# A hand-ordered attention kernel on one core: projections moved ahead of ranks in the front, two score banks lent to projections, rotary factors made later and in two parts, output-weight loads moved

## The chip, the cores and the metric

The kernel runs on one core of one Trainium2 chip. The metric is device time in microseconds (us), the median of several executions. A core has five engines that run side by side, each in its own program order: TensorE (PE) for matrix products, VectorE (DVE), ScalarE (ACT) and GpSimd (POOL) for elementwise work, and SyncE (SP), which here only issues transfers. Transfers (DMA) are issued by an engine's queue and carried by 16 DMA engines. An instruction that waits holds back everything behind it on its engine.

## What is computed

The state x is 64 x 32 x 512, that is 2048 rows of 512 floats, all float32. Four layers are added to it in turn. In outline, with the names of the reference:

```python
def _L0_cond_ref(x, condition, weights):          # channel mix, 32 x 32 per batch
    W = weights[condition]
    return jnp.einsum('bct,bcd->bdt', x, W)
def _L1_cond_ref(...):                            # linear 512 -> 512, plus rank-16 adapters
    result = jnp.einsum('bsd,od->bso', x, base_weight) + base_bias
    h = jnp.einsum('bsd,brd->bsr', x, lora_A_w[adapter_ids])
    return result + jnp.einsum('bsr,bor->bso', h, lora_B_w[adapter_ids])
def _L2_cond_ref(...):                            # attention over a paged cache
    q, k, v = x @ Wq.T, x @ Wk.T, x @ Wv.T        # 32 query heads, 8 key heads, D = 128
    q, k = _rope(_rmsnorm(q, q_norm_w), pos), _rope(_rmsnorm(k, k_norm_w), pos)
    k_all = concatenate([k_cache[block_table], k]); v_all = ...     # 512 + 32 keys
    return (softmax(mask(q @ k_all.T)) @ v_all) @ Wo
x = x + L0(x); x = x + L1(x); x = x + L2(x); x = x + L0(x, other weights)
```

## The kernel before

**Tiles.** The rows are cut into 16 tiles `t` of 128 rows (4 batches of 32). The key heads are cut into two groups `g` of four. A step is one (g, t), so there are 32 steps; two steps with neighbouring t make a `Pair` (16 pairs). A unit is one batch of one step (128 units), and a slot is one key head of one unit: 512 slots, numbered from 0. The work ahead of the first scores has negative slots, from -43 on.

**The order is written by hand.** A plan says for each slot what is recorded there: `at(slot, where, what)`, where `where` is one of fetch, pool, pe, power, turn, dve, keep, act, store. `slot(i)` (L1157 on) records these lists in a fixed order, and each engine runs its instructions in the order in which they are recorded. Around the lists stand the slot's own scores, the transposes of slot i-2 (`flip`) and the products with the values of slot i-3:

```python
run(i, "pe")
run(i, "power")
norm_piece(i)
...
run(i, "turn")
...
run(i, "dve")
norm_piece(i)
norm_piece(i)
run(i, "keep")
```

So in a slot all "pe" products come before all "turn" transposes, and "power" and "dve" are mostly VectorE work. There is no scheduler behind it.

**The front (slots -43 to 0).** `First` carries tile t through the first two layers, with home = -39 + 2t:
- `diagonal` (DVE, home-2) spreads the gathered 32 x 32 channel weights into `mix_diag`; `mix` (PE, home-1) is the channel mix; `add` adds it to x.
- `turn_a`, `keep_a` (home-1, even t): the adapter rows are transposed (aT, L441) and copied by ACT. `turn_x`, `keep_x` (home): x is transposed into x1T (PE) and copied (ACT, L457). `bias` (POOL, home+1).
- `ranks` (PE, home+1) makes h = aT x1T; `own_ranks` (DVE) masks it; `linear` makes the five products into `l_ps`: chunks 0, 1, 2 at home+1, chunks 3 and 4 (the adapter's) at home+2; a second `add` (DVE, L433).
- `turn_out`, `keep_out` (home+3): x2T, the operand of the projections. `sums` (DVE, home+4, odd t) are four sums and differences of a pair's two x2T.
- Beside it, `Turn` transposes the key pages of group 0 ("page turns", 16 of them), `angles()` makes sines and cosines in pieces (`more`: the trig pieces), two a slot, and `rotary(t)` (slots -32 to -17, one tile each) multiplies them by the norm weights into a table in HBM of 256 KB a tile; `v_rows` and `key_f` (row numbers and positions of the cache) are made after slot -38. `rot` has two buffers.

**Projections.** The projections of a pair (keys and values, then query blocks 0 and 1) are written as seven products of sums for each block (`Block.ORDER`), each product two matmuls of 128x128 by 128x512 (L634). Each goes to one PSUM bank (pool `ps_m`, tag m, one buffer); `take` on DVE (L646) adds it to a `raw` tile and frees the bank. Pair i has home = 32(i-1) - 1, products in home to home+30; pair 0 has home -33. For the first pair of a group, `block_sum` (DVE) makes sums of the weights beside it. `Norm` then does RMSNorm, the rotary products (`straight`, `swapped`, L721) and the transposes. `load_rotary` (L579, SP queue, home+6) loads the two tables of a pair.

**Scores and values.** The scores take a pool of two PSUM banks, `ps_s`, first used in slot 0. A unit's keys, `kT`, come in 16 loads of one page, 64 KB each (L777, SP queue), issued at slot 4(u-1) for unit u, into one of two buffers. Its values `v_sb` come by four gathers on POOL's queue; `pen` (POOL, L792) is the mask.

**The end.** In the last pair's slots (home 447) `load_o_weights` (L206) loads the output weights on POOL's queue, eight weights in two halves of 512 KB each; `fetch_o` loads stored attention outputs (o_in: a11, a12, a21, a22, two halves of 512 KB each) from slot 478 on, for three products of the output projection that are done within the last slots. After the last slot, PE does the rest of the output projection (L1283) and the second channel mix (L1301).

## Time and profile before

| | us |
|---|---|
| median of 3 runs | 2508.31 (2504.9 to 2513.72) |
| profiled execution, its time | 2507.74 |
| its span (mean TensorE clock 0.995 of full) | 2506.0 |
| first scores start | 212.81 |
| last slots end, rest of the output projection begins, about | 2200 |

The busy time of each engine by stretch (columns: us of PE, of PE's weight loads, DVE, ACT, POOL, each with its number of instructions; then the granted TensorE clock, the share of the DMA engines and GB/s):

```profile
0.00:50.00 50.00, 33.75 (x110) 19.17 (x111) 26.17 (x54) 9.66 (x14) 21.67 (x33) 0.97 0.71 235
50.00:100.00 50.00, 44.57 (x162) 23.56 (x161) 35.98 (x84) 11.10 (x29) 17.95 (x14) 1.00 0.74 250
100.00:150.00 50.00, 47.22 (x197) 27.26 (x196) 34.46 (x79) 14.96 (x37) 19.85 (x16) 1.00 0.81 263
150.00:200.00 50.00, 46.48 (x182) 25.52 (x180) 29.03 (x56) 17.01 (x55) 16.59 (x18) 1.00 0.62 202
200.00:226.00 26.00, 20.11 (x62) 10.79 (x62) 18.83 (x44) 14.02 (x40) 17.22 (x16) 0.80 0.65 193
226.00:1000.00 774.00, 772.58 (x4637) 582.25 (x4638) 554.86 (x1350) 551.18 (x1651) 414.67 (x329) 1.00 0.65 196
1000.00:2000.00 1000.00, 993.30 (x5931) 746.39 (x5930) 728.51 (x1762) 707.80 (x2127) 546.39 (x437) 1.00 0.63 191
2000.00:2200.00 200.00, 190.37 (x1118) 164.91 (x1117) 105.55 (x209) 71.28 (x180) 67.55 (x67) 0.98 0.55 179
2200.00:2506.00 306.00, 302.20 (x1373) 260.43 (x1371) 95.12 (x129) 2.24 (x6) 9.43 (x10) 1.00 0.26 95
```

A stretch of 50.00 us in which PE is busy 33.75 leaves it 16.25 us without work. In lines of a timeline, further on, the columns are start, duration, engine, line of the code, operation, output <- input by their names in the program, shapes, and in brackets the wait just before it with what ended it. In the list of waits a line names who waited, for whom, and then the sum of the waits in us, their number and the longest.

### The profile page before, as it was taken

What the parts mean: (1) busy time and instruction counts of PE and PEld (TensorE: products, weight loads), DVE (VectorE), ACT (ScalarE), POOL (GpSimd) and SP (SyncE); (2) the same over time, 40 slices, a digit from 0 to 9 for tenths busy, and PEclk for the clock granted to TensorE, in tenths of its full rate; (3) what the DMA queues carried; (4) which work ended last, traced back from release to release, by engine and by line L of the source; (5) the groups of instructions that cost most, each with busy time, mean ns of one, the idle gap of its engine ahead of it and who ended that gap; (6) DMA issues with size and microseconds to landing.
All of it is one profiled execution on the core that took longest, in us unless ns stands there. A gap on an engine that the chain in (4) does not pass through costs nothing.

```text
span 2506.0 us, 47285 instructions
## 1 busy us (share of the span) xinstructions
PE 2450.6 (98%) x13760; PEld 1860.3 (74%) x13760; DVE 1628.5 (65%) x3762; ACT 1399.2 (56%) x4135; POOL 1131.3 (45%) x936
## 2 busy tenths in 40 slices
PE   7998999999999999999999999999999989999999
PEld 3555777777777777767777777777777778888887
DVE  5766777776767677777777677777777756433222
ACT  2235777776767676767767777777776755000000
POOL 4334555555545455645455555555555653000000
PEclk9999999999999999999999999999999999999999
DMA  6775666666666667856665656665656775333221
GB/s 225 266 235 178 193 203 181 199 187 196 191 198 194 187 204 229 257 154 200 181 190 175 186 176 187 182 186 168 191 173 217 229 258 154 122 126 126 87 85 60
DMA packets 442209, 459.71 MB, mean 183 GB/s; under 512 B 50720, under 2 KB 367008, under 8 KB 434144
## 3 DMA queue, kind: packets, MB, share of 16 engines
q1 hardware_dynamic: 392048, 291.76, 37.4%
q0 software_dynamic: 49904, 164.93, 21.6%
q8 instruction: 112, 1.84, 0.3%
q14 instruction: 145, 1.19, 0.2%
HBM read 385.18 MB, written 79.69 MB: 186 GB/s over the span
## 4 chain that ended last, share of the span: by engine, by line
PE 92%; DMA 2%; SPq 2%; issue 1%; DVE 1%; ACT 1%; POOL 0%; DVEq 0%; ACTq 0%
PE proj_ps L634 22%; PE o_ps L876 17%; PE out_ps L1283 15%; PE s_ps L821 10%; PE s_ps L824 8%; PE pT_ps L863 8%; PE head_ps L739 3%; PE l_ps L478 3%; PE o_ps L888 2%; SPq L777 1%; DMA kT<-kT 1%; PE h_ps L462 1%; PE proj_ps L1116 1%; PE s_ps L856 1%; PE mix_ps L1301 1%
## 5 line engine op out<-in xcount | busy, mean ns | idle before, releaser
L105 POOL DMA_INDIRECT v_sb<-v,v_rows x512 | 529.5, 1034 | 360.1 <-PE o_ps L876 251.0
L829 DVE CUSTOM_DVE_ANT_0 sm<-s_ps,pen 128x544 f32<-128x544 f32 x512 | 370.8, 724 | 470.7 <-PE s_ps L824 463.9
L876 PEld LDWEIGHTS o_ps<-pT,v_sb 128*128 128x128 f32 x4096 | 519.7, 192 | 135.2 <-issue 125.0
L840 ACT ACTIVATE sm<-sm,top 128x544 f32<-128x544 f32 x512 | 381.9, 746 | 351.5 <-DVE top L829 351.3
L876 PE MATMUL o_ps<-pT,v_sb 128*128 128x128 f32 x4096 | 542.0, 275 | 3.4 <-DMA v_sb<-v,v_rows 2.0
L846 ACT ACTIVATE sm<-sm,share 128x512 f32<-128x512 f32 x512 | 369.9, 722 | 174.1 <-DVE share L845 173.2
L697 POOL TENSOR_TENSOR rstd<-ss,minus_half 128x4 f32<-128x4 f32 x160 | 208.2, 1301 | 525.8 <-DVE ss L695 525.7
L821 PE MATMUL s_ps<-kT,qT 128*128 128x288 f32 x1024 | 347.3, 421 | 6.2 <-DMA kT<-kT 4.1
L865 DVE COPY pT<-pT_ps 128x512 f32<-128x512 f32 x512 | 351.2, 686 | 1.9 <-PE pT_ps L863 1.9
L824 PE MATMUL s_ps<-kT,qT 128*128 128x256 f32 x1024 | 305.9, 380 | 5.2 <-issue 3.8
L863 PE MATMUL pT_ps<-ident,sm 128*128 128x128 f32 x2048 | 308.1, 273 | 0.0
L863 PEld LDWEIGHTS pT_ps<-ident,sm 128*128 128x128 f32 x2048 | 256.6, 141 | 51.8 <-issue 0.4
L792 POOL TENSOR_SCALAR pen<-key_f,seq_f 128x544 f32<-128x544 f32 x128 | 286.3, 2237 | 10.8
L824 PEld LDWEIGHTS s_ps<-kT,qT 128*128 128x128 f32 x1024 | 194.8, 191 | 60.2 <-issue 4.4
L646 DVE TENSOR_TENSOR raw<-proj_ps,raw 128x512 f32<-128x512 f32 x336 | 225.9, 684 | 12.3 <-PE proj_ps L634 7.3
L690 ACT ACTIVATE sq<-raw 128x128 f32<-128x128 f32 x640 | 197.1, 308 | 33.1 <-DVE raw L646 17.8
L634 PE MATMUL proj_ps<-sum,x 128*128 128x512 f32 x384 | 189.5, 595 | 0.1
L1333 ACT COPY p<-out_ps 128x256 f32<-128x256 f32 x7 | 2.6, 373 | 333.1 <-PE out_ps L1283 333.1
L105 POOL DMA_INDIRECT mix_rows<-in_w,cond_rows x32 | 32.8, 1026 | 314.6 <-DVE mix_diag L171 300.2
L821 PEld LDWEIGHTS s_ps<-kT,qT 128*128 128x128 f32 x1024 | 155.2, 191 | 23.2 <-issue 6.7
L1283 PE MATMUL out_ps<-w,o_in 128*128 128x256 f32 x768 | 167.1, 379 | 0.0
L1283 PEld LDWEIGHTS out_ps<-w,o_in 128*128 128x128 f32 x768 | 145.9, 190 | 19.8
(162 smaller groups left out, 3381.9 us busy)
## 6 DMA issues: line engine op xcount, KB each, us to landing
kT<-kT SPq DMA_DIRECT2D x2048, 64.0 KB
o<-oT SPq DMA_DIRECT2D x29, 1024.0 KB
o_in<-o SPq DMA_DIRECT2D x28, 1024.0 KB
rot<-rot SPq DMA_DIRECT2D x48, 256.0 KB
page_rows<-in_kv_cache SPq DMA_DIRECT2D x32, 256.0 KB
v<-in_kv_cache SPq DMA_DIRECT2D x32, 256.0 KB
kT<-page_rows SPq DMA_DIRECT2D x32, 256.0 KB
vn<-raw SPq DMA_DIRECT2D x32, 256.0 KB
```

The costliest lines, as they stand in the source:

```text
L105: nc.gpsimd.indirect_dma_start(out=dst, out_offset=None, in_=table, in_offset=bass.IndirectOffsetOnAxis(ap=index, axis=0),)
L634: nc.tensor.matmul(self.ps, lhsT=self.pair.x[x][:, c if x == "b" else half.start + c, :], rhs=blocks(self.b)[w][:, c, :], start=(c == 0), ...
L792: nc.gpsimd.tensor_scalar(self.pen, key_f, seq_f[:, self.b : self.b + 1], BIG, ALU.is_ge, ALU.mult)
L821: nc.tensor.matmul(ps[:, first:HID], lhsT=q, rhs=self.kT[:, :n1, k, :], start=True, stop=True)
L824: nc.tensor.matmul(ps[:, HID : first + LA], lhsT=q, rhs=self.kT[:, n1:, k, :], start=True, stop=True)
L829: nc.vector.tensor_tensor_reduce(out=sm, in0=ps[:, first : first + LA], in1=self.pen, scale=1.0, scalar=3e38, op0=ALU.add, op1=ALU.min, ac ...
L840: nc.scalar.activation(sm, sm, AF.Exp, bias=top, scale=-1.0, accum_out=total)
L846: nc.scalar.activation(sm[:, :L], sm[:, :L], AF.Copy, scale=share)
L863: nc.tensor.transpose(ps[:, c, :], self.sm[k][:, c * P : (c + 1) * P], ident)
L865: nc.vector.tensor_copy(pT, ps)
L876: nc.tensor.matmul(self.o_ps[k], lhsT=self.v[c][:, k * D : (k + 1) * D], rhs=self.pT[k][:, c, :], start=(c == 0), stop=False,)
L1283: nc.tensor.matmul(ps[:, :HALF], lhsT=o[:, i, :], rhs=w[i // REP][:, i % REP, :], start=(i == 0), stop=(i == KG * REP - 1),)
```

## The change

It edits four things in the plan, and what goes with them:
1. In the front, a new list "late", recorded after "pe", takes `ranks` and the first three products of `linear`; so in their slot the next tile's `mix` and the projections come before them on PE. The transpose of the adapter rows moves one slot later (`turn_a`, home-1 to home), and the gather of these rows moves to home-3.
2. The rotary tables are made in slots -27 to -19, one to three tiles a slot, and in two parts (q and k), each with its own store and, for later pairs, its own load: k at home+2, q at home+9. For pair 0 they are made in the tiles that the projections read. The trig pieces are spread one or two a slot over slots -40 to -29, and `v_rows` and `key_f` are made after slot -34.
3. In the slots -11 to -3 every second product of a projection goes to the two banks of `ps_s`, which the scores use from slot 0.
4. The last output weights and the early loads of a11 to a22 get other slots.

```diff
--- before
+++ after
@@ -209,7 +209,7 @@
     xS_dram = [dram.tile([P, 2, NC, P], F32, name=f"xS_{p}") for p in range(NT // 2)]
-    rot_dram = [dram.tile([P, 4, D], F32, name=f"rot_{t}") for t in range(NT)]
+    rot_dram = [dram.tile([P, 2, 2, D], F32, name=f"rot_{t}") for t in range(NT)]
...
@@ -370,22 +370,31 @@
-            rot = start_pool.tile([P, 4, D], F32, name="rot", bufs=2)
-            for i, (name, what) in enumerate(
-                (("q", "cos"), ("q", "sin"), ("k", "cos"), ("k", "sin"))
-            ):
-                nc.vector.tensor_tensor(
-                    rot[:, i, :].rearrange("p (a b) -> p a b", a=2),
-                    w_sb["trig"][:, ("cos", "sin").index(what), t, :]
-                    .unsqueeze(1)
-                    .to_broadcast([P, 2, D // 2]),
-                    norm_w[name, what],
-                    ALU.mult,
-                )
-            rot_of[t] = rot
+            if t < 2:
+                step = pair_of[0].steps[t]
+                step.rot = {kind: rotary_tile(kind, t) for kind in "qk"}
+            else:
+                rot = start_pool.tile([P, 2, 2, D], F32, name="rot", bufs=2)
+                rot_of[t] = {"q": rot[:, 0], "k": rot[:, 1]}
+            for kind in "qk":
+                for i, what in enumerate(("cos", "sin")):
+                    nc.vector.tensor_tensor(
+                        (step.rot if t < 2 else rot_of[t])[kind][:, i, :].rearrange(
+                            "p (a b) -> p a b", a=2
+                        ),
+                        w_sb["trig"][:, i, t, :].unsqueeze(1).to_broadcast([P, 2, D // 2]),
+                        norm_w[kind, what],
+                        ALU.mult,
+                    )
+        def rotary_tile(kind, i):
+            return proj_pool.tile([P, 2, D], F32, name=f"rot_{kind}{i}")
         def store_rotary(t):
-            nc.sync.dma_start(out=rot_dram[t], in_=rot_of.pop(t))
+            rot = pair_of[0].steps[t].rot if t < 2 else rot_of.pop(t)
+            for i, kind in enumerate("qk"):
+                nc.sync.dma_start(out=rot_dram[t][:, i], in_=rot[kind])
...
@@ -403,11 +412,13 @@
                     at = slice(self.t // 2, self.t // 2 + 1)
-                    lora["a"] = first_pool.tile([P, HID], F32, name="a_rows")
-                    gather(lora["a"], lora_a, lora["rows"][:, at])
                     lora["b"] = first_pool.tile([P, HID], F32, name="b_rows", bufs=2)
                 self.b_rows = lora["b"]
+            def fetch_a(self):
+                lora["a"] = first_pool.tile([P, HID], F32, name="a_rows")
+                gather(lora["a"], lora_a, lora["rows"][:, self.t // 2 : self.t // 2 + 1])
...
@@ -444,10 +455,11 @@
                 self.turn(lora["a"], "aT", "to")
+                self.ps_of_a = self.ps_of_turn
                 lora["aT"] = first_pool.tile([P, NC, P], F32, name="aT")
-                nc.scalar.copy(lora["aT"], self.ps_of_turn)
+                nc.scalar.copy(lora["aT"], self.ps_of_a)
...
@@ -573,10 +585,12 @@
-            def load_rotary(self):
+            def load_rotary(self, kind):
                 for i, step in enumerate(self.steps):
-                    step.rot = proj_pool.tile([P, 4, D], F32, name=f"rot_{i}")
-                    nc.sync.dma_start(out=step.rot, in_=rot_dram[step.t])
+                    step.rot[kind] = rotary_tile(kind, i)
+                    nc.sync.dma_start(
+                        out=step.rot[kind], in_=rot_dram[step.t][:, "qk".index(kind)]
+                    )
...
@@ -624,12 +638,15 @@
-            def __init__(self, pair, b):
-                self.pair, self.b = pair_of[pair], b
+            def __init__(self, pair, b, slots):
+                self.pair, self.b, self.slots = pair_of[pair], b, slots
                 x, half, w = self.ORDER[i]
-                if c == 0:
+                if c == 0 and i % 2 and self.slots[2 * i] in range(-11, -2):
+                    self.ps = ps_s.tile([P, 2 * HID], F32, name="s_ps")[:, :HID]
+                elif c == 0:
                     self.ps = ps_m.tile([P, HID], F32, name="proj_ps", tag="m")
...
@@ -704,24 +721,24 @@
             def straight(self):
-                which = 2 if self.k is None else 0
+                kind = "k" if self.k is None else "q"
                 self.a = proj_pool.tile([P, REP, D], F32, name="rot_a", bufs=2)
                     self.raw,
-                    self.step.rot[:, which, :].unsqueeze(1).to_broadcast([P, REP, D]),
+                    self.step.rot[kind][:, 0, :].unsqueeze(1).to_broadcast([P, REP, D]),
                     ALU.mult,
             def swapped(self):
-                which = 3 if self.k is None else 1
+                kind = "k" if self.k is None else "q"
                 self.b = proj_pool.tile([P, REP, D], F32, name="rot_b")
                         self.raw[:, :, (1 - i) * half : (2 - i) * half],
-                        self.step.rot[:, which, i * half : (i + 1) * half]
+                        self.step.rot[kind][:, 1, i * half : (i + 1) * half]
                         .unsqueeze(1)
...
@@ -994,7 +1011,9 @@
                 at(home + 4, "store", call, pair_of, 0, "load", "b")
-            at(home + 6, "fetch", call, pair_of, i, "load_rotary")
+            if i:
+                at(home + 2, "fetch", call, pair_of, i, "load_rotary", "k")
+                at(home + 9, "fetch", call, pair_of, i, "load_rotary", "q")
             for b, slots in (
...
@@ -1017,10 +1036,15 @@
                     loads += [(load_q_weights, g + 1, k) for k in range(KG)]
-                places = (6, 11, 16, 21, 29, 34, 31, 27) if g == NG - 1 else (3, 9, 14, 21, 25, 32)
-                for w, load in zip(places, loads):
-                    for j in (0, 1):
-                        at(home + w + j, "store", *load, j, nc.gpsimd)
+                if g == NG - 1:
+                    places = (
+                        (7, 8), (11, 12), (16, 18), (20, 21), (23, 25), (36, 38), (27, 29), (24, 26)
+                    )
+                else:
+                    places = ((3, 4), (9, 10), (14, 15), (21, 22), (25, 26), (32, 33))
+                for slots, load in zip(places, loads):
+                    for j, w in enumerate(slots):
+                        at(home + w, "store", *load, j, nc.gpsimd)
...
@@ -1031,18 +1055,20 @@
+            if t % 2 == 0:
+                at(home - 3 if t else begin, "pool", call, *f, "fetch_a")
-                at(home - 1, "turn", call, *f, "turn_a")
-                at(home - 1, "keep", call, *f, "keep_a")
+                at(home, "turn", call, *f, "turn_a")
+                at(home, "keep", call, *f, "keep_a")
-            at(home + 1, "pe", call, *f, "ranks")
+            at(home + 1, "late", call, *f, "ranks")
-            at(home + 1, "pe", call, *f, "linear", (0, 1, 2))
+            at(home + 1, "late", call, *f, "linear", (0, 1, 2))
...
@@ -1071,8 +1097,9 @@
             at(home + 1, "store", call, turn_of, key, "store")
-            at(begin + 11 + c, "dve", rotary, c)
-            at(begin + 11 + c, "store", store_rotary, c)
+            home = -27 + max(c - 1, 0) * 10 // NT
+            at(home, "dve", rotary, c)
+            at(home, "store", store_rotary, c)
         for u in range(len(units)):
...
@@ -1130,9 +1157,9 @@
             ("a11", (-1, 0)),
-            ("a21", (6, 7)),
-            ("a12", (8, 9)),
-            ("a22", (11, 12)),
+            ("a12", (7, 9)),
+            ("a21", (10, 12)),
+            ("a22", (13, 15)),
         ):
...
@@ -1166,6 +1193,7 @@
             run(i, "pe")
+            run(i, "late")
             run(i, "power")
...
@@ -1210,6 +1238,9 @@
             nc.gpsimd.dma_start(out=lora["bias"], in_=across(base_b, HID))
+            for i in range(begin + 3, begin + 15):
+                for _ in range(1 + (begin + 5 < i < begin + 11)):
+                    at(i, "store", next, more, None)
             for j in (0, 1):
...
@@ -1219,16 +1250,13 @@
                     lora["mask"] = [own_ranks(0), own_ranks(1)]
-                for _ in range(2 if i > begin + 2 else 0):
-                    next(more, None)
-                if i == begin + 5:
+                if i == begin + 9:
                     nc.vector.tensor_copy(seq_f, ints_sb[:, I_SEQ : I_SEQ + B])
                     v_rows = rows_of(const, "v_rows", table, B * NC, PSIZE, lane32_f)
-            assert next(more, "end") == "end"
             for i in range(begin + 11, n + VLAG):
```

More of the change, by code (lines that the diff above doesn't have):

```diff
@@ L548, in __init__ @@
                 self.g, self.t = steps[s]
-                self.qT = {}
+                self.qT, self.rot = {}, {}
         class Pair:
@@ L956, in begin_block @@
         def begin_block(pair, b, slots):
-            block = Block(pair, b)
+            block = Block(pair, b, slots)
             for i in range(7):
@@ L1255, in resid_kernel @@
         assert not plan and not pieces, plan
+        assert next(more, "end") == "end"
     with ExitStack() as l3:
```

## The prediction

> **What bounds the kernel now.** I read the busy shares first, then who waited for whom on TensorE, then the timelines of the stretches where it waits.

> ```profile
> PE 2450.6 (98%) x13760; PEld 1860.3 (74%) x13760; DVE 1628.5 (65%) x3762; ACT 1399.2 (56%) x4135; POOL 1131.3 (45%) x936
> ```

> TensorE is busy for 2450.6 of 2506.0 us. The change leaves its 13760 matmuls as they are, so all it can win is idle time (55.4 us) and time at a lower clock. The waits of PE say where that is:

> ```profile
> PE h_ps L462 <- ACT x1T L457: 8.2, 14, 1.4
> PE mix_ps L424 <- DVE mix_diag L415: 7.8, 1, 7.8
> PE proj_ps L634 <- DVE raw L646: 7.1, 7, 3.7
> PE aT_ps L441 <- ACT x_a L494: 4.8, 7, 0.7
> PE s_ps L821 <- DMA kT<-kT: 4.1, 1, 4.1
> PE s_ps L824 <- issue: 3.8, 1, 3.8
> ```

> Three places: the front (to 193.5 us), the passage to the first scores, and two late key loads (1092 and 2020 us). In the front, this piece of three timelines (PE, DVE, POOL) is the whole argument:

> ```profile
> 71.23 1.02 PE L634 MATMUL proj_ps<-sum,x 128*128 128x512 f32 x2
> 72.08 0.60 PE L441 MATMUL x1T_ps<-ident,x_sb 128*128 128x128 f32 x4
> 73.42 1.16 PE L462 MATMUL h_ps<-x1T,aT 128*128 128x128 f32 x8 [0.73 <-ACT x1T L457]
> 74.41 2.74 PE L478 MATMUL l_ps<-base_sb,x1T 128*128 128x512 f32 x6
> 76.99 1.02 PE L424 MATMUL mix_ps<-x_sb,mix_diag 128*128 128x512 f32 x2
> ...
> 71.50 0.69 DVE L433 TENSOR_TENSOR x_sb<-l_ps,x_sb 128x512 f32<-128x512 f32 x1 [1.53 <-PE l_ps L478]
> 72.90 1.49 DVE L507 TENSOR_TENSOR x<-x_a,x_b 128x256 f32<-128x256 f32 x1
> 74.64 0.28 DVE L415 TENSOR_TENSOR mix_diag<-mix_rows,same 128x128 f32<-128x128 f32 x1
> ...
> 72.77 1.33 POOL L436 TENSOR_TENSOR x_sb<-x_sb,bias_sb 128x512 f32<-128x512 f32 x1 [7.43 <-PE x1T_ps L441]
> ```

> PE turns x1T, sits until ACT has copied it, and runs ranks (h) and linear (l) before mix. mix has its diagonal long before (74.92 against 76.99). In the passage, the chain of waits goes over no matmul:

> ```profile
> 209.78 2.07 DMA kT<-kT
> 211.91 2.42 POOL pen L792
> ...
> 220.69 5.09 DMA v_sb<-v,v_rows
> ```

> And at the end, SP's timeline and two-microsecond stretches (PE busy, PEld, DVE, ACT, POOL, clock, DMA share, GB/s):

> ```profile
> 2002.52 17.69 SPq L777 DMA_DIRECT2D kT<-kT  x16
> ...
> 2018.00:2020.00 2.00, 1.99 (x17) 1.70 (x14) 1.33 (x4) 1.17 (x3) 1.58 (x2) 1.00 0.97 354
> 2020.00:2022.00 2.00, 0.17 (x1) 0.20 (x2) 0.00 (x0) 1.07 (x3) 1.64 (x2) 1.00 1.03 420
> 2028.00:2030.00 2.00, 2.00 (x7) 1.64 (x6) 1.28 (x4) 1.31 (x3) 0.00 (x0) 0.50 1.02 383
> ```

> Sixteen key loads of one unit take 17.69 us to issue; elsewhere 9.3 to 12.6. The DMA engines are full, the keys come late, PE stops, then runs at half clock.

> [...] L507 takes 1.49 us beside POOL's bias, its twin L505 0.42 without it.

> **Part 1: mix and projections ahead of ranks; aT moved.** Steps between starts: mix, one linear product or one projection half 0.86, ranks 1.0, a turn 0.44. After x1T, PE now has mix and mostly a projection (0.86 to 2.6 us) where it waited some 0.9; aT now stands after linear(3, 4), where x_a is long copied. Taken away: up to 8.2 + 4.8.

> Added: mix moves ahead by ranks and three linears (3.6 us), up to the diagonal. On DVE the diagonal (slot home-2, an odd slot) stands behind the add of l_ps and, in every second odd slot, behind the four `sums`. From the end of linear(4) at 71.23 to the start of mix that is 74.92 - 71.23 + 0.07 = 3.8 us, POOL's contention in it. PE has one projection and x1T in between, 1.3: it waits 2.4, where it waited 0.9 before. Behind mix everything on PE is queued. Over four slots from 71.23: after, 3.8 + mix 0.86 + projection 0.86 + ranks 1.0 + linears 2.58 + x2T 0.44 + linears 1.72 = 11.3, then without sums 10.0 (no wait): 21.3. Before it was 93.07 - 71.23 = 21.8. Slots with two projections or page turns wait less, -21, -17 and -13 (a norm piece ahead of the sums) about as long. The same sum for the others comes to between -1.6 and +0.6. I take +0.5 in all for slots -29 to -8, and -0.7 for slot -31, which has a block sum of 1.14.

> Early slots: the trig pieces and v_rows leave slot -38. There L478 waited 2.2 for DVE and then ran 4.47 instead of 2.6. Without these, and with ranks and aT not waiting, linear(4) of t=2 ends at 41.1 instead of 48.5 (base_w still holds the first linear until 19.5): +7.4. But v_rows (27.68 to 30.48), key_f and the block sums now meet in slots -34 and -33: DVE has 11.6 us there, PE 9.6; mix waits 3 to 4 and the clock may fall. From linear(4) of t=2 to that of t=3: 13 to 16 against 12.2; I take -2.

> **Part 2: rotary in slots -27 to -19, in two parts.** 64 products of 0.20 each (start to start) in nine slots instead of sixteen. Behind them on DVE stands the `take` that frees the only projection bank; projections now come 3.6 us earlier in even slots. Slots -26, -24, -20 and -18: at most 2.0 + 1.4 + 1.6 + 0.8 = 5.7; the lower end is 0, as DVE has gaps of up to 3.0 in the trace. I take -3. The stores (two of 0.33 each for one) may hold DVE at the two `rot` buffers: 0 to -3, taken 0. Half clock after the 2.4 us waits: 0 to -8, I take -1, since the clock fell only once in the front before. Front: 7.4 - 2 - 0.7 + 0.5 - 3 - 1 = about +1.

> Later pairs: the q table's load still stands ahead of a unit's keys (slot 232) and still waits for the last q norm, which before held SP for 11.69 us from 1072.64. Only the place against v_new changes: +0.6 of the 4.1. With 256 KB less beside the keys at 1914 us: +0.5 of 1.3.

> **Part 3: two banks ahead of the scores.** It takes away the 5.9 us of L634 between 195 and 208 us. Worth 0: from 193.5 SP issues 32 key loads (to 209.78), then pen and v_sb, to 225.82; PE has nothing urgent. If that cover were gone it would be 5.9.

> **Part 4: output weights and o_in.** Before, in slots 474 to 482, ten weight halves of 512 KB and two of a11; at their densest, 2001 to 2013 us, six. After, one or none in a slot from 463 to 494. The stall costs 1.8 + 3.8 (late keys), 1.5 (a11), 1.0 (v_sb), 0.2, and half the 6 us at half clock: 11.3. Left: slots 483 to 489 still have five halves and the 1 MB store of oT, 3.6 MB in about 25 us or 144 GB/s, beside the 190 of an ordinary stretch; 335 is near the full share. Keys have some 3 us of slack a unit. I leave a new stall of 2 (0 to 9): +9.3. POOL waiting for PE at slots 470 and 471 delays v_sb, which is asked for four slots early: 0.

> **Sum:** 1 + 1.1 + 9.3 = 11.4 us off the span of 2506.0 (its run took 2507.74; median 2508.31): 2497 on the median.

> **The rivals.**
> - The front wins too (as the waits alone would say): DVE frees diagonal and bank before PE asks, so 12 instead of 1: 2486. For it: DVE has only 65%. Against: its order puts the sums ahead of the diagonal.
> - The stall only moves: the loads after slot 483 fill the DMA engines, the keys at 484 and 488 are late again, 1.5 left of 9.3: 2505. For it: 335 GB/s. Against: 2040 to 2052 has four halves and full DMA without a stall.
> - Slower: VectorE gates mix in the front. Place: slots -33 to -13. Price: the 13 us of mix waits and 5.7 of bank waits, with half clock (8) after them, less 9.1 no longer waited for from 58 us on; with early slots +3 this is -15, and the end gives 8: 2515. It decides from a diagonal later than 2.4 us after x1T, or when these waits drop the clock each time.

> **Chances.** Forecast 0.50, front wins 0.20, stall moves 0.13, slower 0.17. A measurement of this kernel tells about 0.3%, 7.5 us. Faster: 0.20 and most of 0.50, 0.67; same: the rest and the moved stall, 0.16; slower 0.17. The forecast's own range is 2490 to 2503; for 8 in 10 it is 2484 to 2514.

> **What would show it.** Right: in the waits of PE, h_ps <- ACT and aT_ps <- ACT nearly gone, mix_ps <- DVE mix_diag of 10 to 15 us in their place; the first scores within 5 us of 212.8; no sixteen key loads over 13 us after 1960; the stall at 1092 still there. Wrong: first scores at 200 or earlier (front wins), or after 220 with a clock below 0.9 in the front (slower), or a new stop of 5 us near slot 486.

## The result and the profile after

The changed kernel takes 2515.91 us (median of 20 runs, 2509.66 to 2520.44) against 2505.87 us for the kernel before in the same sessions (20 runs, 2501.55 to 2513.72). The ratio is 1.0039 (95% interval 1.0031 to 1.0047): slower by 10 us, where 11 us less were forecast. The time lies 2 us above the range. What happened is the rival "Slower: VectorE gates mix in the front", which had a chance of 0.17 and gave 2515.

TensorE's busy time on the page of the changed kernel, first:

```profile
PE 2454.2 (98%) x13760; PEld 1863.4 (74%) x13760; DVE 1626.6 (65%) x3762; ACT 1398.6 (56%) x4135; POOL 1124.8 (45%) x936
```

Its matmuls are as many as before; they took 3.6 us longer, and the span grew by 7.7. The waits of PE in the changed kernel, to be laid beside the list of before:

```profile
PE mix_ps L435 <- DVE mix_diag L426: 28.8, 11, 8.8
PE proj_ps L651 <- DVE raw L663: 11.9, 7, 5.3
PE s_ps L841 <- DMA kT<-kT: 3.7, 3, 2.5
PE s_ps L838 <- DMA kT<-kT: 3.3, 1, 3.3
```

The waits for ACT (h_ps 8.2, aT_ps 4.8) are gone, as forecast. In their place mix waits for its diagonal. The longest of these, 8.8, is the very first mix, which waited 7.8 before; the other ten are new and make 20.0 us. The busy times by stretch (us of PE, PEld, DVE, ACT, POOL with their instruction counts, granted clock, DMA share, GB/s) show where the time went:

```profile
0.00:50.00 50.00, 32.57 (x115) 18.62 (x116) 28.56 (x60) 10.85 (x16) 23.67 (x35) 0.98 0.77 253
50.00:100.00 50.00, 41.69 (x140) 22.37 (x138) 27.97 (x61) 8.23 (x19) 14.46 (x13) 0.92 0.62 199
100.00:150.00 50.00, 42.58 (x161) 23.85 (x162) 31.81 (x85) 11.42 (x32) 16.07 (x13) 0.93 0.78 247
150.00:200.00 50.00, 45.34 (x176) 26.08 (x175) 25.25 (x47) 15.28 (x45) 14.85 (x12) 0.93 0.64 194
...
2000.00:2200.00 200.00, 195.10 (x1167) 167.65 (x1167) 113.64 (x227) 82.44 (x222) 70.91 (x70) 0.99 0.56 180
```

From 50 to 200 us PE is less busy than before (129.6 against 138.3 us), and the clock stands at 0.92 or 0.93 where it was 1.00. From 2000 us on it is busier: there the change wins. Measured along the program: linear(4) of tile 2 starts 6.0 us earlier than before (41.7 against 47.7), of tile 3 only 1.5 earlier, of tile 15 17.7 later (209.3 against 191.6). The first scores start at 227.38 instead of 212.81, 14.6 later; the distance then keeps at 14.7 for 440 slots. At slot 500 it is 6.3, and the span ends 7.7 later. (The rest of the output projection begins at 2122.1 us in the kernel before, not at about 2200 as the table of before has it, and at 2129.2 in the changed one.)

One of the places, the same as the one shown before (tile 6 in mix, t = 5 in x1T), as timelines of PE, DVE and POOL of the changed kernel:

```profile
70.99 1.02 PE L651 MATMUL proj_ps<-sum,x 128*128 128x512 f32 x2
71.85 0.60 PE L452 MATMUL x1T_ps<-ident,x_sb 128*128 128x128 f32 x4
74.74 1.65 PE L435 MATMUL mix_ps<-x_sb,mix_diag 128*128 128x512 f32 x2 [2.29 <-DVE mix_diag L426]
76.18 1.91 PE L651 MATMUL proj_ps<-sum,x 128*128 128x512 f32 x2
77.89 1.29 PE L474 MATMUL h_ps<-x1T,aT 128*128 128x128 f32 x7
...
71.26 0.69 DVE L444 TENSOR_TENSOR x_sb<-l_ps,x_sb 128x512 f32<-128x512 f32 x1 [3.32 <-PE l_ps L490]
71.87 0.41 DVE L516 TENSOR_TENSOR x<-x_b 128x256 f32<-128x256 f32 x1
72.32 0.43 DVE L517 TENSOR_TENSOR x<-x,x_a 128x256 f32<-128x256 f32 x1
72.66 1.49 DVE L519 TENSOR_TENSOR x<-x_a,x_b 128x256 f32<-128x256 f32 x1
74.07 0.41 DVE L520 TENSOR_TENSOR x<-x_a,x 128x256 f32<-128x256 f32 x1
74.41 0.28 DVE L426 TENSOR_TENSOR mix_diag<-mix_rows,same 128x128 f32<-128x128 f32 x1
...
72.54 1.33 POOL L447 TENSOR_TENSOR x_sb<-x_sb,bias_sb 128x512 f32<-128x512 f32 x1 [7.68 <-PE x1T_ps L452]
```

PE stands 2.29 us after x1T, and the projection behind mix stands with it, to 76.18. DVE isn't idle in this time: the add, four sums (one stretched to 1.49 beside POOL's bias) and then the diagonal. So far it is what the prediction worked out (2.4). What it left out is in the durations after the wait: two mix matmuls take 1.65 instead of 1.02, two of the projection 1.91 (from start to start 1.71, from 76.18 to 77.89, where a projection half otherwise takes 0.86). Three stretches of 3.41 us each (same columns as above) say why:

```profile
68.38:71.79 3.41, 3.41 (x12) 1.67 (x11) 0.53 (x1) 0.59 (x1) 0.00 (x0) 1.00 0.36 116
71.79:75.20 3.41, 1.12 (x6) 0.66 (x5) 2.86 (x6) 0.58 (x1) 1.57 (x2) 1.00 0.78 236
75.20:78.62 3.42, 3.42 (x8) 1.74 (x7) 0.00 (x0) 0.00 (x0) 0.71 (x1) 0.50 0.98 338
```

In 71.79 to 75.20 PE was busy 1.12 us of 3.41, and in the 3.41 us after it the granted clock is half. This happened six times between 20 and 200 us, 23.8 us at half clock in all, where it was once (3.4 us) before.

At the end, SP's issues of the changed kernel, and then one of its two-microsecond stretches, beside those of before:

```profile
2002.25 9.37 SPq L794 DMA_DIRECT2D kT<-kT  x16
2015.80 12.77 SPq L794 DMA_DIRECT2D kT<-kT  x16
2030.32 13.17 SPq L794 DMA_DIRECT2D kT<-kT  x16
```

```profile
2032.00:2034.00 2.00, 0.20 (x1) 0.23 (x2) 0.00 (x0) 0.00 (x0) 1.92 (x2) 1.00 0.99 393
```

No sixteen loads take 17.69 us any more, but one unit's still take 13.17 with the DMA engines full (share 0.99 from 2032 to 2034), and one stop of 2.5 us is left.

### The profile page after: what moved, and what is told of

Same layout as the page of the kernel before. It is cut to its first block, busy times and chain, and to the rows that moved or that the text cites. A ratio compares the mean times of both kernels' runs of the same rounds, so it can differ in the third digit from the quotient of the medians.

```text
span 2513.7 us, 47403 instructions
## 1 busy us (share of the span) xinstructions
PE 2454.2 (98%) x13760; PEld 1863.4 (74%) x13760; DVE 1626.6 (65%) x3762; ACT 1398.6 (56%) x4135; POOL 1124.8 (45%) x936
## 3 DMA queue, kind: packets, MB, share of 16 engines
q0 software_dynamic: 49904, 164.93, 21.8%
## 4 chain that ended last, share of the span: by engine, by line
PE 92%; DVE 2%; DMA 2%; issue 2%; SPq 1%; POOL 0%; ACT 0%; DVEq 0%; ACTq 0%
PE proj_ps L651 22%; PE o_ps L893 17%; PE out_ps L1312 15%; PE s_ps L838 10%; PE s_ps L841 8%; PE pT_ps L880 8%; PE head_ps L756 3%; PE l_ps L490 2%; PE o_ps L905 2%; DMA kT<-kT 1%; SPq L794 1%; PE h_ps L474 1%; PE mix_ps L435 1%; PE s_ps L873 1%; PE mix_ps L1330 1%
## 5 line engine op out<-in xcount | busy, mean ns | idle before, releaser
L663 DVE TENSOR_TENSOR raw<-proj_ps,raw 128x512 f32<-128x512 f32 x332 | 223.1, 684 | 10.2 <-PE proj_ps L651 4.7
```

## The experiments

Theory A: the order on PE loses the time, because mix, now ahead of ranks and linear, waits for a diagonal that stands late on DVE, and each such wait halves the clock. Rivals: B, the rotary products in nine slots load DVE; C, the trig pieces and v_rows in later slots; A2, the waits alone, without a cost of the clock. Times are medians, each with its ratio to the kernel before of the same session (2505.85 to 2506.98 us) and, in brackets, the 95% interval of the ratio.

**1. The order undone (no_late).**

```diff
-            at(home + 1, "late", call, *f, "ranks")
+            at(home + 1, "pe", call, *f, "ranks")
-            at(home + 1, "late", call, *f, "linear", (0, 1, 2))
+            at(home + 1, "pe", call, *f, "linear", (0, 1, 2))
```

> The changed kernel with ranks and the first three products of linear recorded before mix and the projections again; all else as changed. Theory A (mix stands first on PE and is gated by its diagonal on DVE, and TensorE's clock halves after each such wait): the waits mix_ps <- DVE mix_diag fall from 28.8 us to the 9 of the very first one, at most two stretches of half clock before 200 us instead of six, first scores at 205 to 213 us instead of 227.4, time 0.992 to 0.998 of the kernel before. Theory B (the rotary products, now in nine slots, load DVE): mix no longer waits but ranks, linear or the projections do, first scores still after 220 us, time 1.001 to 1.005. Theory C (the trig pieces and v_rows moved later cost the front): first scores 218 to 224, most of the loss before 60 us.

Measured: 2491.73 us, 0.9941 (0.9926 to 0.9956); first scores at 203.0. Its waits of PE from 20 to 205 us:

```profile
PE h_ps L474 <- ACT x1T L469: 7.4, 14, 0.8
PE proj_ps L651 <- DVE raw L663: 7.2, 4, 5.3
PE l_ps L490 <- DVE x_sb L444: 1.2, 1, 1.2
```

No mix waits for its diagonal, and one stretch of half clock is left (at the very end of the front). The rest of the change, left in place, is worth 14 us; the order alone costs 24.2 us (2515.91 - 2491.73). B and C are out as main causes: the nine rotary slots and the later trig pieces are still there.

**2. The diagonal first on DVE (diag_first)**, with the order as changed:

```diff
-            at(home - 2, "dve", call, *f, "diagonal")
+            at(home - 2, "power", call, *f, "diagonal")
```

> The changed kernel with the diagonal recorded at the head of the DVE work of its slot (among the adds, ahead of the sums, rotary products and norm pieces), all else as changed. Theory A (the diagonal's place on DVE is the gate): mix waits after the first fall from 20 us to below 6, at most two stretches of half clock before 200 us, first scores at 204 to 214 us, time 0.990 to 0.998 of before. Theory B (DVE as a whole is too loaded in these slots): the wait moves from mix to proj_ps <- DVE raw and h_ps or l_ps, first scores after 220, time 1.000 to 1.005.

Measured: 2500.34 us, 0.9977 (0.9969 to 0.9984), 15.6 less than the changed kernel; first scores at 211.9, mix waits of 3.3 us from 20 to 205. Three stretches of half clock remain, one more than expected. The diagonal's place was the main gate. But 8.6 us stay lost against no_late. The wait proj_ps <- DVE raw is 9.7 us in that stretch, where no_late has 1.9 apart from one wait of 5.3 just ahead of the scores: with mix let go, the projections behind it now wait for the `take`. So a part of theory B holds.

**3. Trig pieces, v_rows and rotary back (early_rot_back)**, order as changed:

```diff
-            home = -27 + max(c - 1, 0) * 10 // NT
+            home = begin + 11 + c
...
+                for _ in range(2 if i > begin + 2 else 0):
+                    next(more, None)
-                if i == begin + 9:
+                if i == begin + 5:
```

> The changed kernel with the trig pieces, v_rows and key_f in their slots of before, and the rotary products one tile a slot in slots -32 to -17 as before (still in two parts); order on PE as changed. Theory A (order on PE and the diagonal): the loss stays for the most part, mix waits of 14 us or more after the first, first scores at 220 to 228 us, time 1.000 to 1.005 of before. Theory B or C (rotary in nine slots, or the later trig pieces and v_rows): first scores at 213 or earlier, time below 0.998.

Measured: 2507.47 us, 1.0004 (0.9995 to 1.0014), first scores at 218.4, mix waits 18.4 us from 20 to 205. So the mix waits don't come from these moves, apart from 1.6 us of the one of tile 4 (4.16 before this edit, 2.55 after it). The first scores lie a little ahead of what theory A asked for (220 to 228). Still 8.4 us come back: the waits for `raw` in that stretch fall from 5.4 to 1.2, and the half clock from 23.8 to 13.6 us, worth 4.2 and about 5.

**4. The same without the order (order_only_undone).**

This run makes the edits of 1 and 3 together.

> As no_late, and also the trig pieces, v_rows, key_f and rotary products in their slots of before: of the front only the two parts of the tables, the banks and the place of the adapter rows stay changed. If the later trig pieces and v_rows win by themselves (5 us between 30 and 40 us in no_late): first scores at 207 to 211 us, against 202.5 in no_late, time 0.9955 to 0.9975 of before. If they and the rotary slots win nothing once the order is undone: within 2 us of no_late, 0.993 to 0.995.

Measured: 2494.6 us, 0.9956 (0.9942 to 0.997), first scores at 205.5. With the order of before, the new slots of trig pieces, v_rows and rotary don't lose: no_late, which has them, is 2.9 us lower (2494.6 - 2491.73), but the two intervals overlap, so that a gain isn't shown. With the changed order they lose 8.4. The move has no price of its own: it depends on what stands first on PE.

**5. Both gates eased (diag_rot)**: the edits of 2 and 3 together.

> The changed order on PE (mix and projections ahead of ranks) with both of its gates eased: the diagonal at the head of the DVE work of its slot, and trig pieces, v_rows and rotary products in their slots of before. Theory A (the order is good where DVE keeps up): mix and bank waits in the front below 8 us together after the first mix, first scores at 203 to 209 us, 0.991 to 0.995 of before. Rival (the order needs more of DVE than it has, wherever the diagonal stands): first scores at 211 or later, 0.996 to 0.999.

Measured: 2496.71 us, 0.9957 (0.9943 to 0.9971), first scores at 209.4. Mix waits are down to 1.7 from 20 to 205 us, but the projections wait 10.6 (7.1 for `raw`, one wait of 3.5 without a visible releaser) and the clock falls four times. (The profiled execution, 2500.33, was the slowest of five.) It lies between both expectations, in time nearer to the rival, in first scores nearer to theory A. The changed order isn't better than ranks first (2494.6 in experiment 4, alike but for the diagonal's place) even where DVE has been eased. By the two traces it saves 8.7 us of waits for x1T (h_ps <- ACT), and gives it back at the bank (10.6 for 1.4, apart from the 5.3 just ahead of the scores that both have) and in the clock (four drops in the front for one).

**6. Useless work in the waits (fill).** Ahead of the waiting mixes, PE makes the transposes of x1T again into the same bank:

```diff
-                for c in range(NC):
+                fill = {3: 9, 4: 3, 5: 5, 6: 6, 7: 5, 8: 3, 9: 3, 10: 3, 11: 5, 13: 5}
+                for c in list(range(NC)) * (fill.get(self.t, 1) if name == "x1T" else 1):
```

> The changed kernel with useless work on PE: ahead of the ten mixes that wait, the transposes of x1T are made two to eight times more into the same bank, 37 groups of 0.44 us, 16 us in all, each less than the wait that follows. Theory A1 (the half clock after a wait is a cost of its own): at most two stretches of half clock before 200 us instead of six, mix still waits for its diagonal but for some 16 us less, first scores at 214 to 220 us instead of 227.4, so 16 us of added work make the kernel faster than the changed one by 7 to 12 us: 0.999 to 1.001 of before. Theory A2 (the waits are the whole loss, and the half clock falls into them): first scores at 226 or later, 1.003 to 1.007 of before.

Measured: 2500.51 us, 0.9977 (0.997 to 0.9983), first scores at 211.6: 16 us of added work made the changed kernel 15.4 us faster, more than theory A1 asked for. One stretch of half clock is left before 200 us. The place of above, PE of fill:

```profile
68.08 1.02 PE L652 MATMUL proj_ps<-sum,x 128*128 128x512 f32 x2
68.94 2.35 PE L453 MATMUL x1T_ps<-ident,x_sb 128*128 128x128 f32 x20
71.12 1.02 PE L435 MATMUL mix_ps<-x_sb,mix_diag 128*128 128x512 f32 x2
71.98 1.02 PE L652 MATMUL proj_ps<-sum,x 128*128 128x512 f32 x2
```

There are twenty transposes instead of four, and mix and projection take 1.02 again. A part of what goes beyond theory A1 shows on DVE, here of fill:

```profile
69.75 0.42 DVE L520 TENSOR_TENSOR x<-x_a,x_b 128x256 f32<-128x256 f32 x1
70.09 0.41 DVE L521 TENSOR_TENSOR x<-x_a,x 128x256 f32<-128x256 f32 x1
70.42 0.28 DVE L426 TENSOR_TENSOR mix_diag<-mix_rows,same 128x128 f32<-128x128 f32 x1
```

POOL's bias waits for the end of the transposes (71.29 here, where the sums end at 70.50), so it now starts after the sums, and the one that took 1.49 takes 0.42. That shows in the trace; no run tried it alone. From 20 to 205 us, work and mix waits are 16.3 + 1.7 = 18.0 us where 20.0 were, the waits of projections 3.2 where 6.3 were, and half clock is 20.4 us less, worth at most 10.2. That makes 15.3, and the first scores are 15.8 earlier. The waits alone would be 5.1, so theory A2 is out.

**7. Half of it (fill_less)**: {3: 6, 5: 3, 6: 4, 7: 3, 9: 3, 11: 3, 13: 3}, 7.9 us.

> As fill, with half of the useless work: 18 groups of 0.44 us, 7.9 us in all, ahead of seven of the mixes, so that in no window of 3.41 us PE idles for over 1.8 us. In the traces so far the half clock came after windows of 3.41 us with 2.1 us or more of idle time, not after those with less than 1.8. If that is what decides: at most two stretches of half clock before 200 us, though the mixes still wait some 1 us each, and the time is that of fill, 0.9967 to 0.9987 of before. If the clock follows the waits themselves, or every us of idle counts alike: three stretches or more remain, 0.999 to 1.004.

Measured: 2504.46 us, 0.9993 (0.9985 to 1.0001); first scores at 218.3; two stretches of half clock, 6.8 us in all, and mix waits of 10.9 us from 20 to 205. The expectation for the clock held, that for the time did not: it isn't as fast as fill. In its trace a part of the slow DVE work is still there: both diagonals that take over 1.3 us in the changed kernel, and four sums of over 1.3 us where the changed kernel has six and fill one. So less is gained beside the clock, which makes it the cleaner measure of the clock. Against the changed kernel, work plus mix waits are 7.9 + 10.9 = 18.8 where 20.0 were, so 1.2 less; the half clock is 17.0 us less, worth at most 8.5; together 9.7. The first scores are 9.1 us earlier, and the median 11.5 us lower.

**8. The control (no_late_fill)**: the work of fill in no_late, where no mix waits.

> A control for fill: no_late with the same 16 us of useless transposes at the same places, where no mix waits for its diagonal. If useless work helps only by keeping the clock up in waits: the front is 12 to 17 us longer than in no_late (first scores at 215 to 220 us), 0.999 to 1.002 of before. If it helps in some other way (engines kept further apart): 0.998 or less.

Measured: 2503.55 us, 0.9985 (0.9979 to 0.9992), 11.8 us more than no_late, first scores at 217.6, 14.7 later (in a profiled execution that was the slowest of 21). The ratio is just below the expected one, the first scores are where they were expected: where nothing waits, 16 us of useless work cost 12 to 15.

**9. The end alone (end_only)**: the kernel before with the changed slots of output weights and o_in.

> The kernel before with the changed slots of the output weights and of the early loads of attention outputs alone. The prediction's part 4: no stop of PE of over 3 us after 1960 us, rest of the output projection begins 8 to 10 us earlier than 2122.1, time 0.996 to 0.997 of before. If that gain in the changed kernel came only with its later keys or its rotary loads in two parts: within 0.999 to 1.001.

Measured: 2501.59 us, 0.9979 (0.9971 to 0.9987), 4.3 us less. The profiled run, its fastest (2494.91), shows the whole of the forecast: the rest of the output projection begins at 2109.3, and the lead over the kernel before grows from 3.4 us at slot 470 to 13.3 at slot 490. (A lead of 3.7 is there at the first scores, 209.1 for 212.8, though the front is the same program: by so much two single traces of one front differ here.) The median of 16 runs shows half of the gain, so the expected time was missed.

**10. The end undone (q12_end_back)** and **11. the q tables three slots later (no_late_q12)**, which is its base:

```diff
-                at(home + 9, "fetch", call, pair_of, i, "load_rotary", "q")
+                at(home + 12, "fetch", call, pair_of, i, "load_rotary", "q")
```

> As no_late, with the q tables of later pairs loaded three slots later (home+12). The prediction said that the stop at 1092 us stays because SP waits in this load for the last q norm and the keys behind it come late. If so: no wait of SP of over 3 us there, no stop of PE at 1080 to 1095 us, 3 to 6 us less than no_late (0.9941): 0.9915 to 0.993 of before. If the stop has another cause (full DMA), or the late table holds up the norms: 0.993 to 0.996.

For the other:

```diff
-                        (7, 8), (11, 12), (16, 18), (20, 21), (23, 25), (36, 38), (27, 29), (24, 26)
+                        (6, 7), (11, 12), (16, 17), (21, 22), (29, 30), (34, 35), (31, 32), (27, 28)
...
-            ("a12", (7, 9)),
-            ("a21", (10, 12)),
-            ("a22", (13, 15)),
+            ("a21", (6, 7)),
+            ("a12", (8, 9)),
+            ("a22", (11, 12)),
```

> As no_late_q12, with the output weights and the early loads of attention outputs in their slots of before. The prediction's part 4 (9.3 us): a stop of PE of some 7 us with half clock near 2000 us comes back, 7 to 10 us more than no_late_q12: 0.9945 to 0.996 of before. Rival (end_only showed 4 us in the median of its runs): 0.993 to 0.9945.

Measured: no_late_q12 2486.85 us, 0.992 (0.9906 to 0.9933), 4.9 less than no_late; no stop at 1080 to 1095 us. SP's queue in the changed kernel and then in no_late_q12, at this place:

```profile
1089.16 9.85 SPq L591 DMA_DIRECT2D rot_q<-rot  x2
1099.82 9.43 SPq L794 DMA_DIRECT2D kT<-kT  x16
```

```profile
1066.62 10.05 SPq L794 DMA_DIRECT2D kT<-kT  x16
...
1078.54 1.15 SPq L591 DMA_DIRECT2D rot_q<-rot  x2
```

The same two loads hold SP for 9.85 us ahead of the keys, or for 1.15 behind them. With the end undone: 2492.11 us, 0.9938 (0.9924 to 0.9952), 5.3 more, and PE stops for keys in one long wait, as its waits from 1990 to 2060 us show, first of q12_end_back and then of no_late_q12:

```profile
PE s_ps L838 <- DMA kT<-kT: 6.7, 1, 6.7
```

```profile
PE s_ps L841 <- DMA kT<-kT: 3.2, 1, 3.2
PE s_ps L838 <- DMA kT<-kT: 1.4, 1, 1.4
```

So the changed end shortens the stops in no_late_q12 (4.6 us for 6.7) and doesn't remove them. The time fits the rival, the length of the stop the forecast. By this run and end_only the end is worth 4 to 5 us in the median.

**12. One bank (q12_one_bank)**: no_late_q12 with all projections in the bank m.

```diff
-                if c == 0 and i % 2 and self.slots[2 * i] in range(-11, -2):
-                    self.ps = ps_s.tile([P, 2 * HID], F32, name="s_ps")[:, :HID]
-                elif c == 0:
+                if c == 0:
```

> As no_late_q12, with all projections in the one bank again. The prediction's part 3 (the waits of the projections ahead of the scores lie beside SP's key loads and POOL, worth 0): the wait proj_ps <- DVE raw grows by some 5 us between 170 and 200 us, but the first scores start within 2 us of 203.5 and the time is within 3 us of no_late_q12: 0.991 to 0.9935 of before. Rival (that cover is gone once the front is shorter, and the banks are worth their 5.9 us): first scores 4 us or more later, 0.9935 to 0.9955.

Measured: 2485.67 us, 0.9914 (0.9901 to 0.9928), first scores at 203.7 against 203.5. The two lent banks are worth nothing. The wait for `raw` was expected to grow by some 5 us without them, and it didn't, as the waits of no_late_q12 and then of this run show:

```profile
PE proj_ps L651 <- DVE raw L663: 8.8, 7, 5.3
```

```profile
PE proj_ps L648 <- DVE raw L660: 9.0, 10, 3.7
```

With the banks it comes in fewer and longer pieces: from 170 us to the scores one of 5.3 us, without them four of 5.6 in all. no_late_q12 and this one, whose intervals overlap, are the fastest kernels here, 20 us below the kernel before and 30 below the changed one.

## Why the prediction was wrong

**The early slots (+7.4, then -2).** Right at first: linear(4) of tile 2 is 6.0 us early. From there to tile 3 it took 16.7 us; 13 to 16 were forecast, against 12.2 before. In this stretch mix waits 4.16 us for its diagonal, and 6.8 us at half clock follow.

**The mix waits.** The mechanism was right, and the size of one wait too (2.4 worked out, 2.29 measured), as was DVE's order as the cause: moving the diagonal alone brought 15.6 us back. The total was low: 10 to 15 forecast, 20.0 measured without the first mix. The tiles whose diagonal stands behind the four sums (4, 6, 8, 10, 12 and 14) wait 15.0 of it. The other 5.0 are waits at tiles 2, 3, 5 and 9; for slots without sums the working of the main stretch had "no wait".

**The clock: the step that failed.** The prediction says: "Half clock after the 2.4 us waits: 0 to -8, I take -1, since the clock fell only once in the front before." The measured number is 23.8 us at half clock instead of 3.4, that is 20.4 more, at most 10.2 us of time, as work at half clock took twice as long here (1.71 for 0.86). In experiment 7, 17.0 of these went, with work and mix waits together nearly unchanged, and the first scores came 9.1 us earlier. The count of before was no ground: between 20 us and the passage its front had a single wait of over 2 us (l_ps <- DVE x_sb, 2.2), and just that one was followed by half clock. Its own end, -8, was near the truth, and so was the rival, which carried just that term ("with half clock (8) after them"). How much the clock would take was an estimate, with no run behind it. In the changed kernel it fell behind a wait of 2.29 us, as the three stretches above and the last section show.

**The bank waits (-3).** 5.4 measured from 20 to 205 us. Their cause was rightly placed: with the rotary products back in sixteen slots they are 1.2.

**Front in sum.** The forecast was +1; measured are -17.7 at the last linear and -14.6 at the first scores. Against no_late the first scores are 24.4 us late (227.4 - 203.0). Of PE's waits ahead of them the passage's 5.3 for `raw` is in both; the others make (20.0 + 5.4 + 0.9) - (7.4 + 1.9 + 1.2 + 0.2) = 15.6. The half clock ahead of them is 30.6 us (23.8 and 6.8 in the passage) against 6.8, for at most 11.9. Together at most 27.5, for 24.4 measured: a part of the half-clock stretches is waiting (PE idles 1.12 of the 6.83 us from 47.90, 0.97 of those from 221.98), not work that takes longer.

**Later pairs (+0.6 and +0.5).** Right in cause: SP waits for DVE in the q table's load (9.1 us by the trace), the keys behind it come late, and with the load three slots later the stop is gone (4.9 us). The change itself won nothing there: PE still waits 4.0 us for 4.1, and half clock lasts 6.8 us instead of 3.4. The stop of 1.3 us at 1914 is gone, worth 1.5.

**Part 3, worth 0.** The number was right, the reason was not, so that is luck. The prediction let the banks take away 5.9 us of waits and other work hide the gain. But the waits stay: the changed kernel still waits 5.3 us for `raw` just ahead of its scores, and by experiment 12 they are about as long with the banks as without (8.8 and 9.0 us). So DVE's `take`, or what it waits for, and not the number of banks sets them; whether other work would have hidden a gain stays untested.

**Part 4 (+9.3).** The mechanism was right, and the two profiles alone show 7.0 from slot 470 to 500 (13.3 to 6.3). As a term of the median it was too large: 5.3 (experiment 10) and 4.3 (experiment 9). It was read off one profiled execution, in which the stop of before had its full length; what the other executions of before do there no trace shows.

**The sum.** 14.6 lost at the first scores and the measured 10 in all leave 4.6 won behind them, in line with 5.3 and 4.3. The forecast had 1 and, with later pairs, 10.4. That the rival's 2515 lies within 1 us is in part luck. It stood on the 2508.31 of three runs, 2.4 above the median of twenty, so it forecast 7 us more where 10 were measured: its mix waits were too low (13 for 20.0) and its end too good (8). Of its signs, first scores after 220 came, a clock below 0.9 did not (0.92 and 0.93 in stretches of 50 us).

## What to carry to other kernels

When work is moved up on the bound engine, take from the other engine's order when each of its operands is made, and price a wait there twice: its length, and the slower clock behind it (here 20.0 us of mix waits, and at most 10.2 for the clock). The count of clock drops in the old profile did not carry over to an order that waits elsewhere. A stop that is seen in one execution can promise more than the median keeps: 9.3 us were worked out from it, and 4 to 5 came.

## What the runs showed of the hardware

These counts are this case's own, from the clock records and PE's matmuls of two traces, the kernel before and the changed one. They say what happened in these two.

Between 20 and 2200 us the granted clock stood at half in four stretches of the kernel before (from 32.27, 202.94, 1097.23 and 2025.66 us) and in nine of the changed one (from 47.90, 75.20, 102.51, 129.82, 157.12, 181.02, 221.98, 1109.44 and 2034.45). Each lasted 3.41, 6.83 or 10.24 us, and within a trace their starts lie multiples of 3.41 us apart (from 47.90 to 75.20 it is 27.31, eight times 3.413). So each trace was cut into windows of 3.41 us that begin where these stretches do, 639 in each.

In the changed kernel waits of 1.60 and 1.09 us, of which 2.29 lie in the window from 126.40, were followed by the drop at 129.82. But its wait of 2.83 us for `raw` that starts at 87.48, the longest that starts between 50 and 205 us, was followed by no drop: it lies in two windows, as these stretches show (columns as above).

```profile
85.44:88.86 3.42, 2.04 (x11) 1.07 (x9) 3.42 (x11) 1.07 (x2) 2.01 (x2) 1.00 0.55 156
88.86:92.27 3.41, 1.96 (x11) 1.49 (x12) 1.39 (x5) 1.61 (x8) 0.42 (x1) 1.00 0.82 228
92.27:95.68 3.41, 3.41 (x13) 1.69 (x12) 3.32 (x11) 0.30 (x1) 2.08 (x2) 1.00 0.80 257
```

The expectation of experiment 7 used such a count, of windows at full clock. Its run had two drops before 200 us, and its longest waits of PE from 20 to 205 us were 2.1 us, one for the diagonal and one for `raw`.
